# Score order in one plan and the place of the result copy in the other, in a fused graph-attention and graph-transformer kernel

## The chip, the cores and the metric

The kernel runs on one core of a Trainium2 chip. The metric is the device time of one execution in microseconds (us), as the median of several runs. In the text TensorE is the matrix engine (PE in the profile), ScalarE the engine that computes exponentials (ACT), VectorE (DVE) and GpSimd (POOL) the elementwise engines, and SyncE (SP) the engine whose queue issues most of the transfers.

## The reference

Two layers work on 3327 nodes with 128 features and a 0/1 adjacency matrix. Layer 0 is a graph attention layer. Layer 1 is the one that takes the time:

```python
q = (x @ Wq.T).reshape(d, n, h)          # d = 128, n = 3327, h = 8
k = (x @ Wk.T).reshape(d, n, h)
v = (x @ Wv.T).reshape(d, n, h)
a = jnp.einsum('dnh,dmh->dnm', q, k) * scale
a = a + spatial_encoding + edge_encoding  # both are adj here
a = jax.nn.softmax(a, axis=2)
out = jnp.einsum('dnm,dmh->dnh', a, v)
out = out.reshape(n, h * d)
return out @ Wo.T
```

So there are 128 attention heads over 3327 x 3327 pairs, with only 8 channels each. Each score needs one exponential, 128 x 3327 x 3327 in all. A residual sum and a layer norm follow each layer.

## The kernel before, in words

**Tiling.** The 128 heads are taken four at a time (32 groups, HG = 4). The 3327 queries are cut into 7 blocks (NBLK) of 476 (the last 472). For each of the 32 x 7 = 224 blocks the 3327 keys pass in 26 tiles (NT) of 127 or 128. For one key tile and one *half* (two heads, h = 0 or 1), two score matmuls (`pair_scores`, L151, recorded as L152) write a PSUM tile `scb` of two banks, 128 x 952 scores. The four heads stand in four different groups of 32 rows of the matrix engine.

**Two ways through the exponential.** Twice the adjacency must be added to the scores. For some key tiles, call them *multiplied*, ScalarE takes the exponential straight from the scores (L1164, 128 x 952) and GpSimd multiplies it with a factor made of the adjacency (L1165). For the others, call them *added*, VectorE adds the adjacency to the scores (L1167, twice, one for each half), and one round later ScalarE takes one wide exponential over both halves in place (`exp_late`, L981 to L986, 128 x 1904).

**PSUM.** The scores of a multiplied key lie in the pool `pe`, which has one buffer; those of an added key in the pool `pd`, which has two. The pool `pv` has one bank, the accumulator `av`. One bank is left for side work.

**Rounds and plans.** A block goes through 26 rounds (NR). `laid` (L927) makes the list of rounds of two plans, and blocks take turns: an even block has the first plan, an odd one the second (`kind`, L741). A group of three key tiles (i, i+1, i+2) makes three rounds, written as (key, half):

```
round A:  (i, 1) multiplied,  (i+1, 0) added
round B:  (i, 0) multiplied,  (i+1, 1) added
round C:  (i+2, 0) added,     (i+2, 1) added
```

The first plan has eight such groups and ends with a pair of rounds A and B for keys 24 and 25. So in an even block round 0 is (0,1), (1,0); round 1 is (0,0), (1,1); round 2 is (2,0), (2,1); round 3 starts the next group with keys 3 and 4. The second plan begins with a round of two adds for key 25, then has the eight groups, and ends with one round in which key 24 is half multiplied, half added. So in an odd block round 3 is (2,0), (2,1), both added.

**The order inside a round** is written out by hand, and each engine gets its instructions in this order:
1. TensorE: the scores of the round's two pairs, in the order of the list (L1152 to L1155). Then perhaps a piece of side work (`work_tensor`, L1156).
2. VectorE, ScalarE and GpSimd: for each pair the add, or the exponential and the multiplication (L1157 to L1168).
3. ScalarE: the wide exponential that the round before left over (L1170).
4. TensorE: `products` (L950) of the key tile that stands LAG = 4 rounds back in `order`: four products of 32 columns, each in two passes, that add into `av` (L956).
5. Side work of the other tiles and layers (`work`, L1180), when a round has room for it.

Because of the lag of four, the last product of a block (key 24) is issued in round 3 of the next block. `products` then also issues the copy of results: VectorE copies `av` to SBUF (`o4`, L966), and four stores to the DRAM tensor `oT` (L970) are put down to be issued on SP's queue two rounds later (`issue`, `tick`). The new block's first product follows in round 4; it needs `av`, which the copy sets free.

## Time and profile before

| | |
|---|---|
| median of 3 runs | 10068.84 us (10068.73 to 10071.29) |
| profiled execution, whole | 10067.05 us |
| its span on the core | 10065.3 us |
| ScalarE, TensorE, VectorE, GpSimd busy | 9914.3, 9418.8, 9195.1, 9185.0 us |
| add of one half (L1167), 7728 times | 1143 ns mean |
| exponential from scores (L1164), 3920 times | 1003 ns mean |
| wide exponential (L986), 3920 times | 1808 ns mean |
| multiplication (L1165), 3920 times | 2238 ns mean |
| copy of results (L966), 224 times | 644 ns mean |

A line of the costliest groups shows the code line, the engine, the operation, what it writes and reads, how often, then busy time and mean duration, then the idle time of the engine just before such instructions and what ended most of that. A line of the timeline shows start in us from the span's start, duration, and the same names; equal neighbours are merged into one line ("x3"), and in brackets stands the idle time before it. A weight load of TensorE is PEld; it overlaps with the matmuls. Ends of matmuls are modelled.

### The profile page before, as it was taken

How to read it: one execution, taken by the hardware profiler on the slowest of the kernel's cores; microseconds unless marked ns; L12 is line 12 of the kernel's file. 1: busy time of each engine (PE TensorE's matmuls, PEld its weight loads, DVE VectorE, ACT ScalarE, POOL GpSimd, SP SyncE). 2: the span in 40 equal slices, each digit the busy share in tenths (PEclk: the TensorE clock that was granted, in tenths of full speed). 3: DMA queues.
4: the chain of work that ended last, by engine and by line, in shares of the span. 5: the costliest groups of instructions: out<-in, count | busy, mean ns of one | idle time of the engine just before them, and what ended most of it. 6: DMA issues, size and time to landing. Idle time of an engine off the chain costs nothing. (4 is left out here: it accounts for less than half of the span.)

```text
span 10065.3 us, 207546 instructions
## 1 busy us (share of the span) xinstructions
PE 9418.8 (94%) x79523; PEld 2994.8 (30%) x79523; DVE 9195.1 (91%) x10554; ACT 9914.3 (99%) x7904; POOL 9185.0 (91%) x4954
## 2 busy tenths in 40 slices
PE   7999999999999999999999999999999999999998
PEld 2233232333233233323332332333333233222222
DVE  7899999999999999999999999999999999888888
ACT  7999999999999999999999999999999999999998
POOL 7999999999999999999999999999999999888887
PEclk8999999999999999999999999999999999999999
DMA  6765656665666656565566656556665665555554
GB/s 194 209 178 178 179 168 183 177 177 167 181 173 172 183 166 189 167 183 170 168 179 187 177 172 178 176 170 178 181 178 175 171 175 168 167 157 167 164 163 132
DMA packets 1399414, 1755.28 MB, mean 174 GB/s; under 512 B 349360, under 2 KB 1386890, under 8 KB 1394312
## 3 DMA queue, kind: packets, MB, share of 16 engines
q1 hardware_dynamic: 1388061, 1739.30, 60.1%
q8 instruction: 626, 10.26, 0.4%
q10 hardware_dynamic: 10347, 2.61, 0.1%
q14 instruction: 380, 3.11, 0.1%
HBM read 1637.49 MB, written 103.93 MB: 173 GB/s over the span
## 5 line engine op out<-in xcount | busy, mean ns | idle before, releaser
L1165 POOL TENSOR_TENSOR e<-e,at 128x952 f32<-128x952 f32 (+1 forms) x3920 | 8723.4, 2238 | 793.4 <-ACT e L1164 737.1
L1167 DVE TENSOR_TENSOR e<-scb,at 128x952 f32<-128x952 f32 (+1 forms) x7728 | 8507.2, 1143 | 801.9 <-PE scb L152 682.1
L986 ACT ACTIVATE e<-e 128x1904 f32<-128x1904 f32 (+3 forms) x3920 | 7088.8, 1808 | 20.1 <-DVE e L1167 5.1
L956 PE MATMUL av<-e,v4b 128*32 128x476 f32 (+1 forms) x46592 | 5839.8, 573 | 162.7 <-DVE o L966 133.9
L152 PE MATMUL scb<-q4b,k4b 32*128 32x476 f32 (+1 forms) x23296 | 3816.0, 486 | 448.7 <-ACT e L1164 381.4
L1164 ACT ACTIVATE e<-scb 128x952 f32<-128x952 f32 (+1 forms) x3920 | 3932.0, 1003 | 76.9 <-PE scb L152 30.0
L152 PEld LDWEIGHTS scb<-q4b,k4b 32*128 32x128 f32 (+1 forms) x23296 | 1763.5, 189 | 5418.3 <-ACT e L1164 3159.6
L956 PEld LDWEIGHTS av<-e,v4b 128*32 128x32 f32 (+1 forms) x46592 | 1010.7, 108 | 1312.6 <-issue 940.5
L241 PE MATMUL bank<-hsb,w 128*32 128x129 f32 (+1 forms) x5200 | 278.3, 286 | 0.0
L326 DVE TENSOR_SCALAR_CACHE_REDUCE dump<-a 128x384 bf16<-128x384 f32 (+2 forms) x468 | 247.4, 529 | 0.6
L308 POOL TENSOR_SCALAR w<-trow,er 128x129 f32<-128x129 f32 x650 | 233.6, 381 | 1.3
L317 POOL TENSOR_TENSOR w<-w,a 128x384 f32<-128x384 f32 (+3 forms) x225 | 209.1, 930 | 0.1
L966 DVE COPY o<-av 128x476 f32<-128x476 f32 (+1 forms) x224 | 144.2, 644 | 5.2 <-PE av L956 5.2
L241 PEld LDWEIGHTS bank<-hsb,w 128*32 128x32 f32 (+1 forms) x5200 | 102.5, 108 | 148.4 <-issue 148.4
L241 PE MATMUL bank<-wo,ot 128*32 128x128 f32 x1600 | 85.2, 285 | 0.0
L409 DVE SCALAR_TENSOR_TENSOR lo<-bank,hi 128x256 fp32r<-128x256 f32 (+1 forms) x200 | 83.0, 415 | 0.0
L402 DVE TENSOR_SCALAR hi<-bank 128x256 fp32r<-128x256 f32 (+1 forms) x200 | 83.0, 415 | 0.0
L241 PE MATMUL bank<-wv,x1T 128*32 128x256 f32 x800 | 63.9, 391 | 0.0
L241 PE MATMUL bank<-wq,x1T 128*32 128x256 f32 x800 | 63.9, 391 | 0.0
L241 PE MATMUL bank<-wk,x1T 128*32 128x256 f32 x800 | 63.9, 391 | 0.0
L502 PE MATMUL bank<-ident,o 128*128 128x128 f32 x225 | 52.0, 304 | 0.0
L290 POOL MEMSET a<- 128x128 f32 (+1 forms) x25 | 5.2, 209 | 44.4 <-DVE dump L326 44.4
(123 smaller groups left out, 650.5 us busy)
## 6 DMA issues: line engine op xcount, KB each, us to landing
at<-in_adjT_dram SPq DMA_DIRECT2D x1536, 476.0 KB
at<-ftd SPq DMA_DIRECT2D x1674, 238.0 KB
at<-in_adjT_dram SPq DMA_DIRECT2D x256, 472.0 KB
at<-ftd SPq DMA_DIRECT2D x279, 236.0 KB
k4b<-kT SPq DMA_DIRECT2D x128, 415.9 KB
q4b<-qT SPq DMA_DIRECT2D x1528, 29.8 KB
at<-in_adjT_dram SPq DMA_DIRECT2D x192, 208.2 KB
at<-in_adjT_dram SPq DMA_DIRECT2D x150, 238.0 KB
```

The source lines that it names most:

```text
L152: nc.tensor.matmul(dst, k4[32 * j : 32 * j + H4, first_key(i) : first_key(i) + 2 * r - 1 : 2], q4[32 * j : 32 * j + H4, :nb], start=True, ...
L241: nc.tensor.matmul(dst[c0:c1], w[:, c0:c1], mov, **kw)
L308: nc.gpsimd.tensor_scalar(w, s["t"][:, :, :T3], -LOWEST, e, op0=ALU.min, op1=ALU.max)
L317: nc.gpsimd.tensor_tensor(w, w, s["a"][n][:, c0 - i0 : c1 - i0, :r], op=ALU.mult)
L326: nc.vector.tensor_scalar(z, a, float(k), None, op0=ALU.is_equal, op1=ALU.add, accum_out=even[:, t, at : at + 1])
L402: nc.vector.tensor_scalar(hi[:r, o : o + QW], s["b"][:r, :QW], scale, None, op0=ALU.mult)
L956: nc.tensor.matmul(s.av[32 * j : 32 * j + 32, : s.w], s.v4[:r, j, i * H1 : i * H1 + 32], e[:r, j, : s.w], start=(s.left == NT - 1), stop=( ...
L966: nc.vector.tensor_copy(o4[:, :w], s.av[:, :w])
L986: nc.scalar.activation(e, e, AF.Exp, scale=2.0)
L1164: nc.scalar.activation(eh, z[:r, :, :w], AF.Exp, scale=2.0)
L1165: nc.gpsimd.tensor_tensor(eh, eh, ah, op=ALU.mult)
L1167: nc.vector.tensor_tensor(eh, z[:r, :, :w], ah, op=ALU.add)
```

## The change

Two orders are changed, each in one round of one plan.

In round 1 of an even block the scores are now issued in reverse: first those of (1, 1), which VectorE reads, then those of (0, 0), which ScalarE reads. The elementwise instructions keep their order. The score tiles are kept in a dictionary by key and half, so that the second loop can find them.

In round 3 of an odd block (`n == LAG - 1`), the call that issues the waiting product, and with it the copy of results, is made between the two adds of key 2, ahead of the one with h = 1. On VectorE the copy so stands before the second add. On TensorE the order in the odd plan stays, since both pairs of scores have been issued by then. On the other engines no instruction of the main loop changes its place; in the first group of heads, one store of a new factor (`ftd`) comes behind the four stores of results on SP's queue, where it stood ahead of them.

```diff
             waiting = []
+
+            def multiply(s, i):
+                waiting.append((s, i))
+                while len(waiting) > LAG:
+                    products(*waiting.pop(0))
...
-                        sc = []
-                        for i, h, z in rnd:
-                            sc.append((pe if z is None else pd).tile([P, 2, 512], F32, name="scb"))
+                        sc = {}
+                        for i, h, z in reversed(rnd) if n == 1 and not odd else rnd:
+                            sc[i, h] = (pe if z is None else pd).tile([P, 2, 512], F32, name="scb")
                             for t in range(2):
-                                pair_scores(sc[-1][: kr[i], t, :w], s.k4, s.q4, i, kr[i], 2 * h + t, w)
+                                pair_scores(sc[i, h][: kr[i], t, :w], s.k4, s.q4, i, kr[i], 2 * h + t, w)
                         work_tensor(g * total + at, n, odd)
-                        for (i, h, at_), z in zip(rnd, sc):
-                            r = kr[i]
+                        between = odd and n == LAG - 1
+                        for (i, h, at_) in rnd:
+                            if between and h == 1:
+                                multiply(s, order[n])
+                            r, z = kr[i], sc[i, h]
...
-                        waiting.append((s, order[n]))
-                        while len(waiting) > LAG:
-                            products(*waiting.pop(0))
+                        if not between:
+                            multiply(s, order[n])
```

## The prediction, made before the changed kernel had run

> **What bounds the kernel now.** I read the busy shares first, then the costliest groups, then the list of who waited for whom, then the timeline of one odd block (109) and the even block behind it (110), engine by engine.

> ```profile
> PE 9418.8 (94%) x79523; PEld 2994.8 (30%) x79523; DVE 9195.1 (91%) x10554; ACT 9914.3 (99%) x7904; POOL 9185.0 (91%) x4954
> ...
> L986 ACT ACTIVATE e<-e 128x1904 f32<-128x1904 f32 (+3 forms) x3920 | 7088.8, 1808 | 20.1 <-DVE e L1167 5.1
> L956 PE MATMUL av<-e,v4b 128*32 128x476 f32 (+1 forms) x46592 | 5839.8, 573 | 162.7 <-DVE o L966 133.9
> ```

> ScalarE is busy for 9914.3 of 10065.3 us, and the change takes nothing off it. So a gain can only come from moments in which ScalarE runs dry. The idle column (20.1 us for L986) hides most of them, because a second activation normally starts before the first has ended. The third row shows TensorE waiting 133.9 us for the copy of results (L966).

> Odd block 109, first ScalarE, then VectorE, then TensorE (start, duration, what, and in brackets the idle time before it):

> ```profile
> 4940.21 1.07 ACT L1164 ACTIVATE e<-scb 128x952 f32<-128x952 f32 x1
> 4941.05 1.92 ACT L986 ACTIVATE e<-e 128x1904 f32<-128x1904 f32 x1
> 4942.73 1.09 ACT L1164 ACTIVATE e<-scb 128x952 f32<-128x952 f32 x1
> 4943.81 1.79 ACT L986 ACTIVATE e<-e 128x1904 f32<-128x1904 f32 x1
> 4945.73 0.96 ACT L1164 ACTIVATE e<-scb 128x952 f32<-128x952 f32 x1
> ...
> 4938.23 2.21 DVE L1167 TENSOR_TENSOR e<-scb,at 128x952 f32<-128x952 f32 x2 [0.23 <-PE scb L152]
> 4940.36 0.64 DVE L966 COPY o<-av 128x476 f32<-128x476 f32 x1
> ...
> 4938.48 1.00 PE L956 MATMUL av<-e,v4b 128*32 128x476 f32 x8
> 4941.06 1.00 PE L956 MATMUL av<-e,v4b 127*32 127x476 f32 x8 [1.13 <-DVE o L966]
> ```

> The second activation starts 0.23 before the first ends (4941.28) and ends 1.69 after it. The fourth starts just when the third ends and ends 1.78 after it. The fifth starts 0.13 after the fourth's end, 4945.60, and ends 1.09 after it, where 0.85 is usual. So **an activation that starts at a gap g from the end of the one before costs g + 0.11 us more than a packed one**, and nothing if g is below -0.11. By this measure, taken end to end over all blocks, ScalarE loses on average 0.11 and 0.23 us in rounds 6 and 7 of an odd block, and 0.24, 0.24 and 0.15 in rounds 2, 3 and 6 of an even one: 0.97 us a pair, 112 pairs, 109 us. That is the ceiling. In the odd block the cause is the 1.13 us hole: the first product of the new block needs the one accumulator, which the copy frees at 4941.00.

> Even block 110, in the same order:

> ```profile
> 4980.30 1.06 ACT L1164 ACTIVATE e<-scb 128x952 f32<-128x952 f32 x1
> 4981.49 1.79 ACT L986 ACTIVATE e<-e 128x1904 f32<-128x1904 f32 x1
> 4983.39 0.96 ACT L1164 ACTIVATE e<-scb 128x952 f32<-128x952 f32 x1
> 4984.25 1.78 ACT L986 ACTIVATE e<-e 128x1904 f32<-128x1904 f32 x1
> ...
> 4988.54 0.97 ACT L1164 ACTIVATE e<-scb 128x952 f32<-128x952 f32 x1
> ...
> 4980.25 1.15 DVE L1167 TENSOR_TENSOR e<-scb,at 128x952 f32<-128x952 f32 x1 [1.18 <-PE scb L152]
> 4981.64 3.26 DVE L1167 TENSOR_TENSOR e<-scb,at 128x952 f32<-128x952 f32 x3 [0.24 <-PE scb L152]
> 4984.82 0.64 DVE L966 COPY o<-av 128x476 f32<-128x476 f32 x1
> ...
> 4979.68 0.49 PE L152 MATMUL scb<-q4b,k4b 32*128 32x476 f32 x4 [0.69 <-ACT e L1164]
> 4981.03 0.90 PE L152 MATMUL scb<-q4b,k4b 32*128 32x476 f32 x4
> 4985.52 1.01 PE L956 MATMUL av<-e,v4b 128*32 128x476 f32 x8 [0.24 <-DVE o L966]
> ```

> In round 1 TensorE stands 0.69 us for ScalarE's buffer, VectorE's scores stand behind that wait, VectorE idles 1.18, and its add ends at 4981.40: ScalarE's wide exponential then starts 0.13 late.

> [...] the four score matmuls at 4979.68 take 0.49 us in all, as one does (486 ns mean). [...] In blocks 1 and 2 the copy did wait for its product, and started 0.05 us after the modelled end.

> **Part 2, the copy between two adds (odd blocks, round 3).** Nothing is added or removed; on VectorE the copy goes ahead of the second add of key 2. Its four stores go out two rounds later on SP's queue, as before; in the first group of heads they pass one factor store, which then issues some 1.4 us later (four stores took 1.37) and is read a group later, so at no cost. TensorE's order in the odd plan is unchanged. In block 109:
> - The first add ends at 4939.38. The copy waits for the product of key 24, 4938.48 + 1.00 = 4939.48, so it starts at about 4939.53 and ends at 4940.17, 0.83 earlier than before. The hole of TensorE shrinks by that much.
> - Queued behind the waiting copy is the second add. It runs from 4940.09 (VectorE's instructions overlap by 0.08) to 4941.23 instead of 4940.44. **This add now becomes the late one**: ScalarE's wide exponential of key 2 needs it, and starts 0.09 after it, as the one at 4943.81 does after its add (ended 4943.72): 4941.32. The activation before it ends at 4941.28, so g = 0.04 and 0.15 us are lost where nothing was.
> - In return: the scores of round 5 start at 4941.33, at ScalarE's release, instead of 4941.99. The adds of key 4 end at 4942.29 and 4943.36; ScalarE wants the second at 4943.86, packed, so no loss. The scores of round 7 start at 4944.8 and ScalarE can have them at 4945.4, wanted at 4945.5: no loss. So 0.11 + 0.23 = 0.34 goes and 0.15 comes: **0.19 us a block**.
> - In 24 of the 112 odd blocks the product of key 24 ends not 0.1 but about 0.36 us after the first add. There the new loss is 0.15 + 0.27 = 0.42, and the block loses 0.08.
> - Sum: 88 x 0.18 - 24 x 0.08 = 14 us (0.18, since a few blocks are a little later than 109).

> **Part 1, VectorE's scores first (even blocks, round 1).** Two score matmuls move ahead of two. They fit into the 0.69 us in which TensorE waits; their buffer was freed by an add two rounds back. ScalarE's own pair still starts at its release, 4979.68, and the products behind it at 4980.10. If that cover were gone, the pair would cost ScalarE's scores 0.42 (the step from one pair to the next), of which packed ScalarE would feel 0.3. Now VectorE's scores take TensorE from 4978.99, where the wait began, and its add ends near 4980.7 instead of 4981.40. The losses of rounds 2 and 3 go: the exponential ends at 4983.04 (before 4983.28), the next score exponential at about 4983.95 (4984.35).
> But **what is late next** doesn't move. VectorE's run of three adds starts at 4981.64 with the scores of round 2, which stand behind products that start at 4980.10 as before. Three adds and the copy follow without a gap to 4985.46, then the first product at 4985.52, then the scores of rounds 5 and 6. So ScalarE, now early, waits: 0.10 for the second add (ended 4983.84), 0.13 for the add behind the copy, and its score exponential of round 6 still can't start before about 4988.53. What was 0.40 ahead ends 0.01 ahead. I take **0 to 3 us for part 1**, and put 0.5 into the sum.

> **Sum.** 14 + 0.5, rounded to 14 us. The profiled execution took 10067.05 us (span 10065.3 and 1.75 around it), 1.8 below the median of 10068.84; 14 off gives 10053 for it and **10055** for the median, 0.14% less.

> **Rivals.**
> - *Both parts pay in full.* If the round-2 scores do come earlier once VectorE's are out of the way, the even block keeps its 0.40: 112 x 0.40 = 45, and 14 to 38 from the odd one: 59 to 83 us, about 9998. For it: TensorE has 6% of slack. Against it: the three adds and the copy stand back to back, and their first start hangs on a release that doesn't move. Half of it (10 to 45 us from part 1) gives 10010 to 10045.
> - *The pushed-back add costs more than the copy returns (slower).* Place: the wait of the copy for key 24's product. If all blocks looked like the 24 late ones, each would lose 0.08, 9 us: 10078. It decides from a copy start 0.19 us later than I take; each further 0.1 us costs 11 us. Against it: 88 blocks have the product 0.09 us after the add.
> - *Nothing that counts.* The new loss equals the two old ones, or ScalarE's earlier arrival in the odd block is given back at round 9, as I expect of the even block: 10060 to 10072.

> **How the numbers follow.** A measurement of this kernel can tell about 0.2%, 20 us, from no change. My forecast (10043 to 10060; the late-block share and the 0.05 us of copy start, either way) gets 0.58, both parts in full or half 0.18, nothing 0.14, slower 0.10. Below 10048.7 lie the 0.18 and 0.08 of my own case: faster 0.26. Over 10089 lies 0.04 of the slower case; the rest, 0.70, is between. The range takes in my case, the nothing case, the half of the slower one up to its 10078, and a third of the half-gain: 10030 to 10078, with 0.83 in it.

> **What would show it.** Right: in odd blocks TensorE's wait for L966 falls from about 1.1 to 0.3 us, the gaps of rounds 6 and 7 close, and a new one of about 0.15 opens at round 4; in even blocks the gap at rounds 2 and 3 is gone, and ScalarE loses again at rounds 4 to 6. The wait of products for the copy falls from 133.9 to about 60 us. Wrong: if the even block's round-6 exponential starts earlier against the block's first, part 1 pays; if the odd block's round-4 gap is over 0.34 us, part 2 costs.

## The result and the profile after

| | before | after |
|---|---|---|
| median (19 runs each, taken in turn on one chip) | 10068.69 us (10063.9 to 10072.5) | 10049.58 us (10047.06 to 10053.32) |
| span of the profiled execution | 10065.3 us | 10050.6 us |
| ScalarE busy | 9914.3 us | 9897.6 us |

The ratio is 0.9982, with a 95% interval of 0.9974 to 0.9989: 19.1 us faster, between 11 and 26. The two profiled spans differ by 14.7 us. In what follows, a sum over a trace is held against a difference of spans, and a median against medians.

From the groups of the changed kernel. The lines of code have moved: the wide exponential is now L991 (before L986), the exponential from scores L1172 (L1164), the add L1175 (L1167).

```profile
PE 9477.4 (94%) x79523; PEld 3013.9 (30%) x79523; DVE 9188.5 (91%) x10554; ACT 9897.6 (98%) x7904; POOL 9177.2 (91%) x4954
...
L991 ACT ACTIVATE e<-e 128x1904 f32<-128x1904 f32 (+3 forms) x3920 | 7095.9, 1810 | 26.4 <-DVE e L1175 11.1
L956 PE MATMUL av<-e,v4b 128*32 128x476 f32 (+1 forms) x46592 | 5843.8, 573 | 99.0 <-DVE o L966 68.0
```

Two things are to be seen. The wait of the products for the copy has halved, from 133.9 to 68.0 us. And the wide exponential now has 11.1 us of idle time put down to VectorE's adds, where it had 5.1: a wait has been exchanged for another.

The timeline of odd block 109, changed kernel: ScalarE, then VectorE, then TensorE, as in the prediction.

```profile
4933.47 1.08 ACT L1172 ACTIVATE e<-scb 128x952 f32<-128x952 f32 x1
4934.62 1.79 ACT L991 ACTIVATE e<-e 128x1904 f32<-128x1904 f32 x1
4936.31 0.95 ACT L1172 ACTIVATE e<-scb 128x952 f32<-128x952 f32 x1
4937.16 1.78 ACT L991 ACTIVATE e<-e 128x1904 f32<-128x1904 f32 x1
4938.84 0.96 ACT L1172 ACTIVATE e<-scb 128x952 f32<-128x952 f32 x1
...
4931.51 1.15 DVE L1175 TENSOR_TENSOR e<-scb,at 128x952 f32<-128x952 f32 x1 [0.24 <-PE scb L152]
4932.81 0.65 DVE L966 COPY o<-av 128x476 f32<-128x476 f32 x1 [0.15 <-PE av L956]
4933.38 3.25 DVE L1175 TENSOR_TENSOR e<-scb,at 128x952 f32<-128x952 f32 x3
...
4933.52 1.00 PE L956 MATMUL av<-e,v4b 127*32 127x476 f32 x8 [0.32 <-DVE o L966]
```

The copy starts 0.15 us after the first add's end (4932.66) and ends at 4933.46, and the hole of TensorE in front of the new block's first product is 0.32 us instead of 1.13. The second add (first of the "x3") waits behind the copy, so the wide exponential of round 4 starts at 4934.62, which is 0.07 after the end of the one before it (4934.55). By the prediction's measure that loses 0.18 us. The three activations behind it are packed; rounds 6 and 7 lose nothing any more.

The timeline of even block 110, changed kernel, ScalarE, VectorE, TensorE:

```profile
4973.39 1.07 ACT L1172 ACTIVATE e<-scb 128x952 f32<-128x952 f32 x1
4974.23 1.91 ACT L991 ACTIVATE e<-e 128x1904 f32<-128x1904 f32 x1
...
4978.67 0.94 ACT L1172 ACTIVATE e<-scb 128x952 f32<-128x952 f32 x1
4979.70 1.79 ACT L991 ACTIVATE e<-e 128x1904 f32<-128x1904 f32 x1
4981.63 0.97 ACT L1172 ACTIVATE e<-scb 128x952 f32<-128x952 f32 x1
...
4974.73 3.26 DVE L1175 TENSOR_TENSOR e<-scb,at 128x952 f32<-128x952 f32 x3 [1.04 <-PE scb L152]
```

The wide exponential of round 2 starts 0.23 us before the end of the one ahead of it: the loss there is gone. But the run of three adds still starts 1.34 us after the score exponential of round 1 (before: 4981.64 - 4980.30, also 1.34), the wide exponential of round 5 comes 0.09 late, and the score exponential of round 6 0.14 late. From the start of the exponential of round 1 to that of round 6 it is 4981.63 - 4973.39 = 8.24 us. Before, it was 4988.54 - 4980.30 = 8.24.

The same over the whole run. For each instruction of ScalarE I take the time from the end of the one before to its own end, less what a packed one takes (0.853 us from scores, 1.680 wide), and sum by round. Blocks 0 and 1 are left out, and so is the exponential of half the width that stands at the head of each even block. In us:

| round | before | after | second round's scores alone | copy alone |
|---|---|---|---|---|
| even 2, 3 | 26.8, 26.6 | 0.1, 21.3 | 0.0, 15.3 | 26.9, 28.8 |
| even 5, 6 | 0.7, 15.8 | 19.9, 34.1 | 20.4, 34.1 | 0.5, 16.2 |
| odd 4 | 1.5 | 28.3 | 1.0 | 28.6 |
| odd 6, 7 | 12.5, 27.0 | 0.2, -0.2 | 12.8, 27.2 | 0.3, -0.2 |
| all even rounds | 74.5 | 78.5 | 72.8 | 75.2 |
| all odd rounds | 43.7 | 26.2 | 43.6 | 27.3 |
| sum | 118.2 | 104.6 | 116.4 | 102.5 |

The sum falls by 13.6 us, the span by 14.7. All of the gain lies in odd blocks. In even blocks the losses have only moved: round 2 loses nothing any more, round 3 a little less than before, and rounds 5 and 6 some 37 us more. On the whole even blocks lose 4 us more than before; that goes with six drops of TensorE's granted clock to 0.50 (20 us), as the end of the fifth experiment shows.

### The profile page after: what moved, and what is told of

It reads as the page before. It is cut to its first block, busy times and chain, and to the rows that moved or that the text cites. A ratio compares the mean times of both kernels' runs of the same rounds, so it can differ in the third digit from the quotient of the medians.

```text
span 10050.6 us, 207550 instructions
## 1 busy us (share of the span) xinstructions
PE 9477.4 (94%) x79523; PEld 3013.9 (30%) x79523; DVE 9188.5 (91%) x10554; ACT 9897.6 (98%) x7904; POOL 9177.2 (91%) x4954
## 4 chain that ended last, share of the span: by engine, by line
ACT 41%; PE 21%; POOL 16%; issue 13%; DVE 7%; DMA 2%; SPq 1%; POOLq 0%; ACTq 0%; DVEq 0%
ACT e L991 29%; POOL e L1173 15%; ACT e L1172 11%; PE av L956 11%; PE scb L152 9%; DVE e L1175 5%; PE bank L241 1%; DVE o L966 1%; DMA q4b<-qT 1%; DMA at<-in_adjT_dram 1%; POOL w L308 0%; SPq L733 0%; POOL w L317 0%; DMA k4b<-kT 0%; POOL at L793 0%
## 5 line engine op out<-in xcount | busy, mean ns | idle before, releaser
L1175 DVE TENSOR_TENSOR e<-scb,at 128x952 f32<-128x952 f32 (+1 forms) x7728 | 8499.4, 1142 | 769.7 <-PE scb L152 650.1
L991 ACT ACTIVATE e<-e 128x1904 f32<-128x1904 f32 (+3 forms) x3920 | 7095.9, 1810 | 26.4 <-DVE e L1175 11.1
L956 PE MATMUL av<-e,v4b 128*32 128x476 f32 (+1 forms) x46592 | 5843.8, 573 | 99.0 <-DVE o L966 68.0
L152 PE MATMUL scb<-q4b,k4b 32*128 32x476 f32 (+1 forms) x23296 | 3882.4, 486 | 440.8 <-ACT e L1172 361.9
L1172 ACT ACTIVATE e<-scb 128x952 f32<-128x952 f32 (+1 forms) x3920 | 3921.1, 1000 | 74.9 <-PE scb L152 36.7
L152 PEld LDWEIGHTS scb<-q4b,k4b 32*128 32x128 f32 (+1 forms) x23296 | 1779.3, 189 | 5459.2 <-ACT e L1172 3161.5
L956 PEld LDWEIGHTS av<-e,v4b 128*32 128x32 f32 (+1 forms) x46592 | 1014.1, 109 | 1239.9 <-issue 933.4
L966 DVE COPY o<-av 128x476 f32<-128x476 f32 (+1 forms) x224 | 145.2, 648 | 31.3 <-PE av L956 30.4
```

What stands on the lines that cost most here:

```text
L152: nc.tensor.matmul(dst, k4[32 * j : 32 * j + H4, first_key(i) : first_key(i) + 2 * r - 1 : 2], q4[32 * j : 32 * j + H4, :nb], start=True, ...
L956: nc.tensor.matmul(s.av[32 * j : 32 * j + 32, : s.w], s.v4[:r, j, i * H1 : i * H1 + 32], e[:r, j, : s.w], start=(s.left == NT - 1), stop=( ...
L966: nc.vector.tensor_copy(o4[:, :w], s.av[:, :w])
L991: nc.scalar.activation(e, e, AF.Exp, scale=2.0)
L1172: nc.scalar.activation(eh, z[:r, :, :w], AF.Exp, scale=2.0)
L1175: nc.vector.tensor_tensor(eh, z[:r, :, :w], ah, op=ALU.add)
```

## The experiments

My theory was that of the prediction: the copy's place carries the gain, less a new loss in round 4, and the scores' order gains nothing, because the run of adds that follows hangs on a release that it doesn't move. The rivals were that both parts pay, or that they pay only together. Each edit is against the changed kernel unless it says otherwise, and each median is given beside that of the kernel before from the same session.

### 1 and 2: each part alone

`scores_only` leaves the copy where it was:

```diff
-                        between = odd and n == LAG - 1
+                        between = False
```

> Part 1 alone: in round 1 of even blocks VectorE's scores go first, and the copy of results stays behind both adds in odd blocks. My theory (the gain of part 1 is given back at the run of three adds and the copy, which starts with the scores of round 2): no change, 10062 to 10074 us; ScalarE loses nothing in round 2 of even blocks any more, but the same sum as before over rounds 2 to 6. Rival (part 1 carries a share of the 19 us): 10055 to 10061 us. Second rival (with the scores apart TensorE's clock drops more often, and part 1 costs): 10073 to 10078 us.

Measured: 10067.88 us (13 runs) against 10069.16, ratio 0.9999 (0.9991 to 1.0007).

`copy_only` takes the new order of scores back:

```diff
-                        for i, h, z in reversed(rnd) if n == 1 and not odd else rnd:
+                        for i, h, z in rnd:
```

> Part 2 alone: the copy stands between the two adds of round 3 of odd blocks, and the scores of even blocks keep their old order. My theory (all of the gain is here: the 0.34 us of rounds 6 and 7 go, about 0.2 us come at round 4): 10045 to 10056 us, the same as both parts together within 4 us. Rival (both parts share the gain): 10057 to 10064 us.

Measured: 10054.58 us (21 runs) against 10069.16, ratio 0.9986 (0.9979 to 0.9993), span 10048.2.

So the scores alone do nothing that can be told, and the copy alone brings 14.6 us. The two right-hand columns of the table above say the same by round. Both parts together were measured 5 us below the copy alone, in another session and within both intervals, while the spans stand the other way round (10050.6 and 10048.2). Whether part 1 adds a few us beside part 2 stays open.

### 3: one product of the old block one round earlier

If the even block is held by the chain "scores of round 2, three adds, copy, first product", moving that chain's start forward should let part 1 pay. In `product_one_round_earlier` the round 0 of an even block issues two products, so that none stands between the scores of rounds 1 and 2. The last product of the old block, and the copy with it, stay in round 3:

```diff
-            def multiply(s, i):
+            def multiply(s, i, lag=LAG):
                 waiting.append((s, i))
-                while len(waiting) > LAG:
+                while len(waiting) > lag:
...
-                            multiply(s, order[n])
+                            multiply(s, order[n], LAG - (n == 0 and not odd and g + b > 0))
```

> Both parts, and in round 0 of each even block two products of the block before are issued instead of one, so that none stands between the scores of round 1 and those of round 2. My theory says that the scores of round 2 then start about 0.7 us earlier, with them the run of three adds and the copy, and that the even block keeps what part 1 gave and gave back: about 0.4 to 0.5 us a block, 45 to 55 us in all, 9993 to 10010 us. Rival (something else sets round 6, such as GpSimd's multiplications or the side work): within 8 us of both parts together, 10042 to 10058 us.

Measured: 10035.46 us (6 runs) against 10069.16, ratio 0.9968 (0.9956 to 0.998). That is 14 us below the changed kernel, and about a third of what I expected. Counted from the start of round 1's score exponential, as in all such medians below, the run of adds of an even block starts 0.33 us earlier than in the changed kernel and the copy 0.31 earlier. The losses of rounds 5 and 6 went, from 19.9 and 34.1 to 0.4 and 2.9 us, so the chain behind the second-round scores is what made them. But rounds 2 and 3 lost again (19.3 and 27.8). The two products of round 0 take 1.78 us in block 110:

```profile
4968.24 1.78 PE L956 MATMUL av<-e,v4b 128*32 128x476 f32 x16
```

So TensorE reaches round 1 late. VectorE's scores start 0.08 us after ScalarE has released its buffer, that is after the end of its exponential of round 0, where in the changed kernel they start 0.74 ahead of that (medians): most of the slot in which they could go first is used up. I had moved work out of one full place into another.

### 4: the copy ahead of both adds

This puts a price on an add that waits behind the copy. The odd block's first add of key 2 is pushed back too:

```diff
-                            if between and h == 1:
+                            if between and h == 0:
```

> Both parts, but in odd blocks the copy stands ahead of both adds of round 3. My theory prices a pushed-back add by what ScalarE then waits: the second add ends near 11.2 us after the reference instead of 10.1, ScalarE's wide exponential starts 1.1 us after it could, and 0.9 us a block are lost against the kernel before: about 10165 us (10130 to 10190). Rival (ScalarE's slack covers a pushed-back add, and what counts is only how early the copy frees the accumulator): 10040 to 10070 us.

Measured: 10304.32 us (4 runs) against 10069.16, ratio 1.0234 (1.0218 to 1.025). The direction is as expected, the size more than twice. Round 4 of odd blocks loses 145.7 us, 1.30 a block, about as priced. But rounds 5, 6 and 7 lose 37.6, 26.7 and 84.3, where I had expected the return of the earlier copy.

The timeline of one odd block of this kernel (ScalarE, VectorE, TensorE), and then its windows view: stretch, length, busy time of PE, PEld, DVE, ACT, POOL with counts, granted TensorE clock, DMA share, GB/s.

```profile
5137.88 1.78 ACT L991 ACTIVATE e<-e 128x1888 f32<-128x1888 f32 x1 [1.13 <-DVE e L1175]
5140.53 0.96 ACT L1172 ACTIVATE e<-scb 128x944 f32<-128x944 f32 x1 [0.88 <-PE scb L152]
...
5136.88 0.76 PE L152 MATMUL scb<-q4b,k4b 32*128 32x472 f32 x2 [1.50 <-DVE e L1175]
...
5138.00 1.80 PE L956 MATMUL av<-e,v4b 127*32 127x472 f32 x8
```

```profile
5133.29:5136.70 3.41, 2.09 (x14) 0.58 (x14) 1.86 (x4) 3.41 (x4) 2.92 (x2) 1.00 0.93 310
5136.70:5140.11 3.41, 3.23 (x22) 1.20 (x22) 2.17 (x3) 1.83 (x2) 2.21 (x1) 0.50 0.60 176
```

The first ScalarE line is the price that I had worked out: 1.13 us of idle time for the add. The second, 0.88 us for TensorE's scores, I had not. The same eight products that take 1.00 us elsewhere take 1.80 here. In the windows view TensorE's clock is granted at 0.50 from 5136.70 on, after a window in which TensorE was busy for 2.09 of 3.41 us (here the low clock lasts two windows, 6.8 us). Between 0.5 and 10 ms, 71 such drops (331 us in all) stand in this trace, against 2 (7 us) in the kernel before.

The blocks without a drop show the price by itself: 34 of the 111 odd blocks counted have no low clock in them or in the 3.5 us ahead of them, and they lose 1.31 us each, 1.26 of it in round 4. In the kernel before such blocks lose 0.32, so the step is 1.0 us, where I had expected 0.9. The other 77 lose 3.26 each, and nearly all of the losses in rounds 5 to 7 are theirs. So the granted clock is the part that my price lacked.

### 5: the products of the even block one round later

The other way to move the second-round scores forward: in rounds 1 and 2 of even blocks one more product is kept back. Round 1 issues none, round 2 the one that round 1 put off, and round 3 two. (`multiply` takes its lag as in experiment 3, here and below.)

```diff
-                            multiply(s, order[n])
+                            multiply(s, order[n], LAG + (n in (1, 2) and not odd and g + b > 0))
```

> Both parts, and in even blocks the products of rounds 1 and 2 each go one round later, so that the scores of rounds 2 and 3 are issued ahead of the product that stood before them. Nothing now stands between ScalarE's scores of round 1 and VectorE's of round 2. My theory: VectorE's add of key 1, early by part 1, lets the run of three adds start about 0.9 us earlier, the copy comes about 0.3 us earlier, and of the 0.7 us an even block still loses some 0.2 are left: 45 to 55 us less than both parts together, 9995 to 10015 us. Rival (the copy, now behind two products in one round, is late): 10045 to 10065 us.

Measured: 10075.67 us (13 runs) against 10068.56, ratio 1.0006 (0.9997 to 1.0014). The expectation failed, and yet its mechanism is in the trace. From the end of round 1's score exponential to that of round 6's, the median even block takes 7.88 us, where the changed kernel takes 8.13. That is 0.25 a block, 28 us over 112 blocks, about half of what I expected. The run of adds starts 1.07 us earlier than in the changed kernel and the copy 0.28 (medians; 0.9 and 0.3 expected). But 29 of 111 even blocks are over 8.6 us (in the changed kernel 9); on average they take 2.2 us more than the median block. Even block 64 of this kernel, in the windows view (columns as above), three windows of 3.41 us in a row:

```profile
2938.28:2941.69 3.41, 3.38 (x40) 1.33 (x38) 3.12 (x5) 3.41 (x4) 3.41 (x6) 1.00 0.34 127
2941.69:2945.10 3.41, 2.31 (x20) 0.82 (x18) 3.34 (x7) 3.41 (x4) 3.41 (x3) 1.00 0.76 218
2945.10:2948.51 3.41, 3.41 (x20) 0.64 (x20) 1.70 (x2) 2.98 (x3) 3.41 (x2) 0.50 0.58 200
```

With no product left between the scores of rounds 1 and 2, TensorE is busy for 2.31 of 3.41 us in the middle window, and in the next one its granted clock is 0.50: two products, 1.78 us in experiment 3, take 3.25 here.

```profile
2945.55 3.25 PE L956 MATMUL av<-e,v4b 128*32 128x476 f32 x16
```

This trace holds 27 drops, 113 us of low clock in records of 3.413 us, some of two in a row. The 82 even blocks clear of low clock, in the sense of experiment 4, lose 0.22 us each (in the changed kernel 0.54); the other 29 lose 2.66.

With that, all traces of this study can be asked the same: cut each into windows of 3.413 us, the length of its shortest clock records, in step with those records, take the busy share of TensorE in each window that had its clock granted at 1.00, and see whether the next was granted 0.50. Over twelve traces, between 0.5 and 10 ms:

| TensorE busy in the window | followed by a clock of 0.50 | not |
|---|---|---|
| under 0.55 | 13 | 0 |
| 0.55 to 0.65 | 89 | 33 |
| 0.65 to 0.75 | 63 | 445 |
| 0.75 to 0.85 | 15 | 1290 |
| over 0.85 | 0 | 31200 |

So all 180 drops counted followed a window under 0.85 busy. In the traces before and after, all clock records start a whole number of windows apart, to within 0.02 us. In the changed kernel, drops stand at 8695.2, 9050.2 and 9405.2 us: 355 us apart, which is 8 blocks and 104 windows.

In the changed kernel itself, drops are few: 6, of 20 us in all, against 2 before. One of them, in even block 48 (windows view, columns as above):

```profile
2220.17:2223.58 3.41, 2.59 (x24) 0.96 (x22) 3.40 (x7) 3.41 (x4) 2.83 (x3) 1.00 0.61 177
2223.58:2226.99 3.41, 3.41 (x22) 0.66 (x20) 1.28 (x2) 2.88 (x3) 3.41 (x2) 0.50 0.75 248
```

All six fall in rounds 1 and 2 of an even block, and each makes its block 0.7 to 1.2 us longer. That is enough to account for the 4 us that even blocks lose on the whole: the 103 even blocks clear of low clock lose 0.54 us each, a little less than the 0.57 of such blocks before, and the median even block is 0.01 us shorter.

### 6: the same without the new order of scores

Experiment 5 with part 1 taken back. In this place part 1 should matter, since nothing else holds the scores of round 2.

```diff
-                        for i, h, z in reversed(rnd) if n == 1 and not odd else rnd:
+                        for i, h, z in rnd:
...
-                            multiply(s, order[n])
+                            multiply(s, order[n], LAG + (n in (1, 2) and not odd and g + b > 0))
```

> The kernel with the products of rounds 1 and 2 one round later, but with the scores of round 1 in their old order (part 1 taken back). My theory (part 1 was worth nothing only because products stood before the scores of round 2): the second pair of round 2 now waits for an add that ends near 9.4 us after the reference instead of 8.6, and TensorE with it; at least 45 us slower than with part 1, 10050 to 10110 us. Rival (part 1 is worth nothing here either): within 8 us of the kernel with part 1.

Measured: 10182.81 us (4 runs) against 10068.56, ratio 1.0121 (1.0106 to 1.0137): 107 us above experiment 5, more than twice the least that I expected, and above the range that I gave, as experiment 5 itself was. The count of drops is nearly the same, 28 against 27 (140 us of low clock against 113), so it isn't mainly these that make the difference: even blocks clear of low clock lose 0.97 us each, against 0.22. The median even block takes 8.66 us between the two ends named above, 0.78 more than in experiment 5. **The same edit that is worth nothing in the changed kernel is worth some 90 us where the chain behind it moves with it** (0.79 us a block in the mean, 112 blocks; the spans differ by 90.5). In both kernels it lets VectorE's add of round 1 start about 0.75 us earlier (medians over even blocks). In the changed kernel, held against the copy alone, the run of adds and the copy then start no more than 0.01 earlier. Here the run of adds starts 0.75 earlier, the copy 0.81 and the score exponential of round 6 0.78.

### 7: the odd block's scores earlier

The new loss in round 4 comes from the copy's wait for the product of key 24, and from the add behind it. In `early_scores_in_odd`, TensorE issues the first pair of round 3's scores ahead of the product of round 2, and the product of key 24 ahead of the second pair:

```diff
+                        if odd and n == LAG - 2:
+                            score(early, *rounds[n + 1][0])
                         if not between:
                             multiply(s, order[n])
...
                             if between and h == 1:
                                 multiply(s, order[n])
+                                score(sc, i, h, at_)
```

(`score` makes the tile and issues its two matmuls; the loop over the round's scores leaves out the pairs that are made so.)

> Both parts, and in odd blocks the first pair of scores of round 3 is issued ahead of the product of round 2, the product of key 24 and the copy ahead of the second pair. My theory of the new loss at round 4 (the copy waits for the product of key 24, and the second add behind it): the product of key 24 now ends 0.4 us earlier, the second add near 9.65 us after the reference instead of 10.1, and the loss of 0.15 to 0.4 us at round 4 goes: 24 to 28 us less than both parts together, 10020 to 10028 us. Rival (ScalarE's wide exponential waits there for something else): 10044 to 10056 us.

Measured: 10031.38 us (5 runs) against 10068.56, ratio 0.9962 (0.9948 to 0.9975), 18 us below the changed kernel (21 by the spans), a little less than the 24 to 28 expected. The loss of round 4 fell from 28.3 to 7.8 us, nearly all of the difference. Odd block 109 of this kernel (its line numbers: L1180 is the exponential from scores, L1183 the add), ScalarE, then VectorE:

```profile
4923.65 1.07 ACT L1180 ACTIVATE e<-scb 128x952 f32<-128x952 f32 x1
4924.49 1.91 ACT L991 ACTIVATE e<-e 128x1904 f32<-128x1904 f32 x1
...
4922.57 0.65 DVE L966 COPY o<-av 128x476 f32<-128x476 f32 x1
```

The copy no longer waits for its product (no bracket), and the wide exponential of round 4 starts 0.23 us before the end of the one ahead of it: packed.

### 8 and 9: two changes together

`both_orders` is 5 and 7 together; the place where the two meet:

```diff
+                        if odd and n == LAG - 2:
+                            score(early, *rounds[n + 1][0])
                         if not between:
-                            multiply(s, order[n])
+                            multiply(s, order[n], LAG + (n in (1, 2) and not odd and g + b > 0))
```

> Both of these orders together: products of rounds 1 and 2 one round later in even blocks, early scores in odd blocks. If the two add up: 9968 to 9990 us. If ScalarE's time saved in one block is given back in the other: 9995 to 10010 us.

Measured: 10044.01 us (10 runs) against 10068.56, ratio 0.9976 (0.9967 to 0.9986). It is 32 us below experiment 5 (22 by the spans), so the odd block's part adds up; but 25 drops remain (109 us of low clock). The expectation was written before experiment 5 had shown its drops, and it missed: by 54 us where the two add up, and by 34 where they don't.

`earlier_product_and_early_scores` is 3 and 7 together, shown in the same place:

```diff
+                        if odd and n == LAG - 2:
+                            score(early, *rounds[n + 1][0])
                         if not between:
-                            multiply(s, order[n])
+                            multiply(s, order[n], LAG - (n == 0 and not odd and g + b > 0))
```

> Both parts, two products in round 0 of even blocks, and in odd blocks the early first pair of scores of round 3. Neither order made TensorE's clock drop more often by itself. If they add up: 14 and 18 us off both parties' 10050, so 10012 to 10022 us. If one gives back what the other gains: 10028 to 10036 us.

Measured: 10012.93 us (5 runs) against 10067.39, ratio 0.9945 (0.9931 to 0.9959), as expected if the two add up, with one drop ahead of the last block. This is the best version found: 54 us below the kernel before, 37 below the changed one. ScalarE still loses 68.8 us in it by the measure of the table, 59.0 of them in even blocks, mostly in rounds 2 and 3.

### 10: the best version without the new order of scores

Experiment 9 with part 1 taken back; against experiment 9 the diff is:

```diff
-                        for i, h, z in reversed(rnd) if n == 1 and not odd else rnd:
+                        for i, h, z in rnd:
```

> The same kernel with the scores of round 1 of even blocks in their old order (part 1 taken back). My theory: with two products in round 0 TensorE reaches round 1 only when ScalarE has released its buffer, so both pairs start together whichever is first, and part 1 does nothing: within 5 us of the kernel with part 1. Rival (part 1 still lets VectorE start earlier): 10 us or more slower than with it.

Measured: 10030.86 us (5 runs) against 10067.39, ratio 0.9962 (0.9949 to 0.9976). My theory fell: I had expected the order to be worth next to nothing here, since TensorE reaches round 1 only at ScalarE's release, and it is worth 18 us. Counted from the end of round 1's score exponential, VectorE's add of round 1 starts 0.05 us later without it in the median even block, and what follows stands 0.05 to 0.06 later, some 6 us over 112 blocks; the loss of even round 2 goes from 19.4 to 31.9 us. In the mean over even blocks the add starts 0.11 later and the score exponential of round 6 0.17, which is the whole difference (19 us), so some blocks carry far more of it than others. Seven drops against one are part of that; how the rest divides stays open.

## Why the prediction was right, point by point

- **The time.** Forecast 10055, measured 10049.58; for the profiled execution 14 us less, measured 14.7. What lies between the two medians' 19.1 and the 14 is within the interval (11 to 26). That the sum came out so close is in part luck: by the table odd blocks gained 17.5 us where 14 was forecast, and even blocks lost 4.0 where a gain of 0.5 was.
- **Part 2, the return.** Forecast 0.11 + 0.23 us a block in rounds 6 and 7. Measured: 12.5 + 27.0 us before and nothing after, 0.35 a block. The hole of TensorE was to be 0.30 in block 109 and is 0.32.
- **Part 2, the new late one.** The second add did become the late one, and round 4 the place. Forecast 0.15 us in 88 blocks and 0.42 in 24, 23 us in all. Measured: 28.3 us, 25 blocks with 0.52 on average (one of them, with 1.66, stands at a clock drop; without it 0.47), the rest with 0.18. So the term was a fifth too small: the exponential starts 0.07 after the one ahead of it in block 109, not 0.04. Small gains in rounds 1, 5 and 10 of odd blocks (some 3 us) made up for it.
- **Part 1.** Forecast 0 to 3 us, 0.5 taken. Measured: 0.01 us gained by the median even block, as in "ends 0.01 ahead". The loss of round 2 moved to rounds 5 and 6. Two signs on the list were wrong: round 4 stayed clean (-0.1 us), and the loss of round 3 did not go but fell from 26.6 to 21.3 us. Half of what is left there belongs to the 8 even blocks with low clock. The other half is 0.10 us a block, the wait for the second add that the working itself had priced at 0.10. The wait of the products for the copy fell to 68.0 us; forecast 60.
- **What the prediction lacked: TensorE's clock.** It took matmul durations as given. In this change that cost only some 4 us, for 6 drops, but the risk stood on its weak side: the same kind of edit in experiment 5 lost all its 28 us, and more, with 27 drops (113 us of low clock). The waits alone don't show that risk: the longest single wait of TensorE ahead of the drop was 1.50 us in block 111 of experiment 4, and 0.49 in block 48 of the changed kernel.
- **The rivals.** *Both parts pay in full* is ruled out by experiment 1 (0.9991 to 1.0007 for part 1 alone). What spoke against it, the adds and the copy back to back behind a release that stays, is what experiments 3, 5 and 6 show: move that chain, and rounds 5 and 6 lose next to nothing (experiment 3), or the same order is worth 90 us (6 against 5). *The pushed-back add costs more* did not come to pass; with one add behind the copy it cost 0.25 us a block and the copy returned 0.35, with both adds it cost 1.30. *Nothing* held for part 1 and not for part 2.

## What to carry to other kernels

Where an engine is bound, an earlier start is worth what it is still worth at the next fixed release: follow the gain on to the first wait that hasn't moved, and put it down as nothing if it ends there (the new order of scores: nothing that can be told in experiment 1, some 90 us in 6 against 5). A copy that frees a shared accumulator can go ahead of an add when it returns more than the add then costs (here 0.35 against 0.25 us a block with one add behind it, but 1.30 with two); count what is queued behind it with the same care as what it frees. When an order is changed on TensorE, look at the granted clock as well as at the waits, in windows as short as its records (here 3.413 us): in experiment 5 the order gained 0.25 us in the median even block, 28 us in all, and 29 even blocks took on average 2.2 us more than the median block, 64 us.
